# A graph layer's edge bookkeeping with one operand of each VectorE instruction in PSUM

## The chip, the cores and the metric

The kernel runs on one core of one Trainium2 chip. The metric is the device time of one execution in microseconds; before the change the median of three runs is 3950.51 us (3949.45 to 3950.6).

## What is computed

12,500 nodes with 128 features each and 200,000 edges, sorted by their destination. A node's row is normalized and passed through a relu; two graph layers follow, and their result is added to x:

```python
w = edge_weight_raw / jnp.maximum(wsum, EPS)[dst]
feat = jax.nn.relu(node_features @ W_pool + b_pool)
msg = feat[src] * w[:, None]
neigh = jax.ops.segment_max(msg, dst, num_segments=N)
...
rst = node_features @ W1_self + neigh @ W1_neigh + b1
...
h = jax.nn.relu(rst)
msg2 = h[src] * w[:, None]
neigh2 = jax.ops.segment_sum(msg2, dst, num_segments=N) / jnp.maximum(deg, 1.0)[:, None]
out = jax.nn.relu(h @ W2_self + neigh2 @ W2_neigh + b2)
```

Layer 1 takes the largest message of each destination, layer 2 their mean. The sums over a destination's edges (wsum, deg) and the places where one destination ends and the next begins have to be found from dst.

## The kernel before

The edges are cut into 391 groups of 512 (the last has 320), and 128 groups stand in one tile, so there are NT = 4 tiles of [128, 512]: one row of a tile is one group. The program has three stages.

**Preparation.** A loop over 25 sets of four 128-row node tiles, 28 turns with i from 0 to 27, is pipelined by hand. In one turn VectorE adds the bias of set i-3 (`fb`, line 388), forms the reciprocal and offset of set i-1 (403, 405) and the statistics of set i (420, 421); ScalarE normalizes (`xn`, line 409, four instructions), takes the square root (423) and copies the transposed set into `hT` (396); PE transposes (411) and multiplies by W_pool (399); GpSimd does the relu (`fr`, 391); SP stores the rows in the table `feat_d` in HBM (392). Between turns the loop draws single steps from generators: the edge work of tile 0 (`edges1`, one step per turn from i=2), loads, and `sources` (371, 374), which lays the source indices out as `srcT`.

**Layer 1** is a loop over groups, again pipelined by hand. In turn i GpSimd issues up to four gathers (`indirect_dma_start`, line 525), each of 128 rows of `feat_d` by a column of `srcT`; their tiles `gt` come from a pool of eight buffers. In every twelfth group one chunk of 128 rows is fetched row by row from the queues of SP and ScalarE instead (`Rows`, lines 459 to 517, tile `ga`). ScalarE scales the rows by the edge weight (`gs`, 654), PE transposes them into `pm` (655), VectorE runs the maximum along each row with a scan (661: `pm` in PSUM, `kt` in SBUF) in which `kt`, a broadcast row of `keep_d`, cuts the run at a new destination. Lines 669 and 670 draw pairs together, 678 builds a selection matrix, 685, 698, 703 and 710 place the result in `agg`, and `nodes1` (555 to 580) turns a finished node tile into rows of `h_d`, the table of layer 2.

Beside that loop runs the **edge work**: `edges1` (tiles 1 to 3; tile 0 was done in the preparation), `edges2`, `edges3`, `fitness` for all four tiles, and `verdict`, in that order. `edges1` marks where a destination goes on (`goes`) and ends (`last`), writes `keep_d`, sums the weights of each destination with two scans (231, 239: the second starts from the carry of the row before), and forms `ewT`, `lastT`, `invT` and `bases`. `edges2` counts edges, forms the place within the window (`locT`) and the reciprocal of weight times count; `edges3` scans backwards and forms `w2T`, the weights of layer 2; `fitness` tests whether the edge list suits the fast path. Each is a generator; a `yield` ends a step. The lists of steps are worked off by `side_step`, one step at a time, at the end of each odd turn:

```python
            if i % 2:
                side_step()
```

A job with a due turn is finished at once when its turn has come; everything else is due at turn 391. Each VectorE operation of these jobs works on [128, 512] or half of it; nearly all two-input ones read two tensors in SBUF. The only PSUM tile that they use is `pq`, of which the preparation has two buffers and layer 1 one.

**Layer 2** gathers rows of `h_d` with the same line 525 and sums them with matmuls (759) whose weights come from `locT` and `w2T`.

[...]

Of the kernel before, what the change touches and what calls it, by code (L numbers as in the profile page):

```python
# [8 lines left out]
BF16 = mybir.dt.bfloat16  # L9
# [3 lines left out]
AF = mybir.ActivationFunctionType  # L13
OP = mybir.AluOpType
AX = mybir.AxisListType
# [3 lines left out]
P = 128  # L19
D = 128  # L20
G = 512
Q = 4
# [13 lines left out]
def gnn_kernel(ctx, tc, x, src, dst, ew, w_pool, b_pool, w1s, w1n, b1, w2s, w2n, b2, out):  # L36
# [155 lines left out]
    def work(name, n=G, dtype=F32):  # L192
        return rp.tile([P, n], dtype, name=f"r_{name}")

    def columns(get, f, n):

        pt = get()
        for j in range(n):
            nc.tensor.transpose(pt[:, j, :], f[:, j * P:(j + 1) * P], ident)
        return pt[:, :n, :]  # L200

    def carried(get, a, t, near, wrap, step):

        pe = get()[:, 0, 0:1]
        nc.tensor.matmul(pe, shift[near], a[:, t + 1:t + 2], start=True, stop=False)
        nc.tensor.matmul(pe, shift[wrap], a[:, t + 1 + step:t + 2 + step], start=False, stop=True)
        return pe

    def backwards(a):
        return bass.AP(tensor=a.tensor, offset=a.offset + G - 1, ap=[list(a.ap[0]), [-1, G]])  # L210

    def pairs(a):
        return a.rearrange("p (c two) -> p c two", two=2)

    def edges1(get, t):

        before, cur, behind = (dr[:, t, i:i + G] for i in range(3))
        begin = work("first", 1)
        nc.vector.tensor_copy(begin, cur[:, 0:1])
        pe = get()[0:1, 0, :]  # L220
        nc.tensor.matmul(pe, begin, ident, start=True, stop=True)
        goes = work("goes", dtype=BF16)
        nc.vector.tensor_tensor(goes, cur, before, OP.is_equal)
        keep = work("keep", dtype=BF16)
        nc.vector.tensor_scalar(keep, goes, 1.0, -NEG, op0=OP.subtract, op1=OP.mult)
        nc.sync.dma_start(keep_d[t * P:(t + 1) * P, :], keep)
        yield
        nc.vector.tensor_copy(bases[0:1, t * P:(t + 1) * P], pe)
        pt = columns(get, er[:, t, :], Q)
        fw = work("f0")  # L230
        nc.vector.tensor_tensor_scan(fw, goes, er[:, t, :], 0.0, op0=OP.mult, op1=OP.add)
        nc.vector.tensor_copy(sums[:, t + 1:t + 2], fw[:, G - 1:G])
        yield
        nc.scalar.activation(ewT[:, t], pt, AF.Copy)
        pe = carried(get, sums, t, "up", "up_wrap", -1)
        yield
        first = work("first", 1)
        nc.vector.tensor_copy(first, pe)
        nc.vector.tensor_tensor_scan(fw, goes, er[:, t, :], first, op0=OP.mult, op1=OP.add)
        yield  # L240
        last = work("last", dtype=BF16)
        nc.vector.tensor_tensor(last, cur, behind, OP.not_equal)
        yield
        nc.vector.tensor_tensor(er[:, t, :], fw, last, OP.mult)
        yield
        loc = work("f1")
        nc.vector.tensor_tensor(loc, cur, cur[:, 0:1].to_broadcast([P, G]), OP.subtract)
        yield
        nc.vector.scalar_tensor_tensor(loc, loc, 1.0, last, op0=OP.add, op1=OP.mult)
        yield  # L250
        two, inv = fw[:, :G // 2], fw[:, G // 2:]
        nc.vector.tensor_tensor(two, pairs(loc)[:, :, 0], pairs(loc)[:, :, 1], OP.max)
        nc.vector.tensor_tensor(inv, pairs(er[:, t, :])[:, :, 0], pairs(er[:, t, :])[:, :, 1], OP.add)
        yield
        nc.vector.tensor_scalar(inv, inv, TINY, None, op0=OP.max)
        pt = columns(get, two, Q // 2)
        yield
        nc.vector.reciprocal(inv[:, :G // 4], inv[:, :G // 4])
        yield
        nc.scalar.activation(lastT[:, t], pt, AF.Copy)  # L260
        yield
        nc.vector.reciprocal(inv[:, G // 4:], inv[:, G // 4:])
        pt = columns(get, inv, Q // 2)
        yield
        nc.scalar.activation(invT[:, t], pt, AF.Copy)

    def edges2(get, t):

        before, cur, behind = (dr[:, t, i:i + G] for i in range(3))
        goes = work("goes", dtype=BF16)  # L270
        nc.vector.tensor_tensor(goes, cur, before, OP.is_equal)
        yield
        fw = work("f0")
        nc.vector.tensor_tensor_scan(fw, goes, ones_r, 0.0, op0=OP.mult, op1=OP.add)
        nc.vector.tensor_copy(counts[:, t + 1:t + 2], fw[:, G - 1:G])
        yield
        pe = carried(get, counts, t, "up", "up_wrap", -1)
        loc = work("f1")
        nc.vector.tensor_tensor(loc, cur, cur[:, 0:1].to_broadcast([P, G]), OP.subtract)
        yield  # L280
        first = work("first", 1)
        nc.vector.tensor_copy(first, pe)
        nc.vector.tensor_tensor_scan(fw, goes, ones_r, first, op0=OP.mult, op1=OP.add)
        pt = columns(get, loc, Q)
        yield
        nc.scalar.activation(locT[:, t], pt, AF.Copy)
        yield
        nc.vector.scalar_tensor_tensor(fw, er[:, t, :], TINY, fw, op0=OP.max, op1=OP.mult)
        yield
        for j in range(Q):  # L290
            nc.vector.reciprocal(fw[:, j * P:(j + 1) * P], fw[:, j * P:(j + 1) * P])
            yield
        last = work("last", dtype=BF16)
        nc.vector.tensor_tensor(last, cur, behind, OP.not_equal)
        yield
        nc.vector.tensor_tensor(er[:, t, :], fw, last, OP.mult)

    def edges3(get, t):

        cur, behind = (dr[:, t, i:i + G] for i in (1, 2))  # L300
        stays = work("goes", dtype=BF16)
        nc.vector.tensor_tensor(stays, cur, behind, OP.is_equal)
        yield
        bw = work("f0")
        nc.vector.tensor_tensor_scan(backwards(bw), backwards(stays), backwards(er[:, t, :]), 0.0,
                                     op0=OP.mult, op1=OP.add)
        nc.vector.tensor_copy(heads[:, t + 1:t + 2], bw[:, 0:1])
        yield
        pe = carried(get, heads, t, "down", "down_wrap", 1)
        yield  # L310
        first = work("first", 1)
        nc.vector.tensor_copy(first, pe)
        nc.vector.tensor_tensor_scan(backwards(bw), backwards(stays), backwards(er[:, t, :]), first,
                                     op0=OP.mult, op1=OP.add)
        pt = columns(get, bw, Q)
        yield
        nc.vector.tensor_tensor(w2T[:, t], pt, ewT[:, t], OP.mult)

    def fitness(get, t):

        before, cur, behind = (dr[:, t, i:i + G] for i in range(3))
        begin = cur[:, 0:1]
        wrong = work("goes", dtype=BF16)
        nc.vector.tensor_tensor(wrong, cur, before, OP.is_lt)
        yield
        nc.vector.tensor_reduce(bad[:, t, 0:1], wrong, axis=AX.X, op=OP.max)
        yield
        loc = work("f1")
        nc.vector.scalar_tensor_tensor(loc, cur, float(N - 1), begin.to_broadcast([P, G]),
                                       op0=OP.min, op1=OP.subtract)  # L330
        yield
        nc.vector.tensor_scalar(wrong, loc, float(LW - 1), None, op0=OP.is_gt)
        yield
        nc.vector.tensor_reduce(bad[:, t, 1:2], wrong, axis=AX.X, op=OP.max)
        yield

        one = work("first", 1)
        nc.vector.tensor_tensor(one, before[:, 0:1], behind[:, G - 1:G], OP.is_equal)
        real = work("real", 1)
        nc.vector.tensor_scalar(real, begin, float(PAST), None, op0=OP.is_lt)  # L340
        nc.vector.tensor_tensor(bad[:, t, 2:3], one, real, OP.mult)
        nc.vector.tensor_tensor(bad[:, t, 3:4], begin, need[:, t:t + 1], OP.is_lt)
        yield

        last = work("last", dtype=BF16)
        nc.vector.tensor_tensor(last, cur, behind, OP.not_equal)
        yield
        nc.vector.tensor_tensor(wrong[:, :G // 2], pairs(last)[:, :, 0], pairs(last)[:, :, 1], OP.mult)
        nc.vector.tensor_reduce(bad[:, t, 4:5], wrong[:, :G // 2], axis=AX.X, op=OP.max)

    def verdict(get):
        all_bad = work("first", 1)
# [30 lines left out]
    for i in range(len(groups) + 3):  # L383
# [29 lines left out]
        if at[0]:  # L413
# [9 lines left out]
            nc.scalar.activation(rstd, mv[:, :, 1], AF.Sqrt, bias=eps)  # L423
            offs[i] = ps.tile([P, Q], F32, name="neg")
            nc.vector.tensor_scalar(offs[i], mv[:, :, 0], -1.0, None, op0=OP.mult)
        if 2 <= i < 20:
            next(first_edges, None)
        if i >= 6:
            next(rest, None)
# [174 lines left out]
    with tc.manual_schedule(), tc.tile_pool(name="ew", bufs=3) as wk, \  # L604
# [33 lines left out]
        for i in range(max(turn) + 6):  # L638
# [72 lines left out]
                                     stop=j == len(chunks) - 1)  # L711
            node_stage(2)
            byrow.rows(i, nc.scalar)
            if i % 2:
                side_step()
        assert not busy
        i = NG
# [168 lines left out]
```

## Time and profile before

| what | value |
| --- | --- |
| median of 3 runs | 3950.51 us |
| the profiled execution's own time | 3949.8 us |
| its span | 3947.9 us |
| first and last gather of layer 1 | 91.9 and 2023.9 us |
| first and last gather of layer 2 | 2045.8 and 3936.5 us |
| busy: PE, PE weight loads | 55%, 45% of the span |
| busy: VectorE, ScalarE | 42%, 20% |
| busy: GpSimd | 75% |
| mean granted TensorE clock | 0.529 |
| DMA: bytes moved, mean rate | 295.43 MB, 75 GB/s |

A row of the profile's groups gives line, engine and operation, what is written and read by the program's names, the shapes and the count; then the busy time in us and the mean duration in ns; then the idle time of the engine just before, and what ended most of it. GpSimd's busy time does not count the time in which it issues: "issue" stands for a pause in which the engine waited for nothing that the profile shows. In the timeline a row begins with the start in us from the span's start and the duration in us; the bracket tells how long the engine was idle before it, and what ended that. In the chain of work that ended last, each piece has a start and a duration, and is followed by what it released.

### The profile page before, as it was taken

Reading aid. Unit: us, or ns where it says so; the run is one execution under the profiler, and the core shown is the slowest. Engines: PE = TensorE matmul, PEld = TensorE weight load, DVE = VectorE, ACT = ScalarE, POOL = GpSimd, SP = SyncE. Lnnn points to the kernel's source line nnn. Section 1 sums busy time; section 2 is a strip of 40 time slices with the busy share of each in tenths; the row PEclk is TensorE's granted clock in tenths of the full one; section 3 lists DMA queues with packets and bytes.
Section 4 is the critical chain, followed back from the end, with each engine's and each line's share of the span. In section 5 each row is a group of like instructions: output and inputs, shape, how many; then the busy total and the mean of one; then the engine's idle time right before and its main releaser. Section 6 shows DMA issues by size and latency. Waiting matters only on the chain.

```text
span 3947.9 us, 55088 instructions
## 1 busy us (share of the span) xinstructions
PE 2163.9 (55%) x8349; PEld 1764.2 (45%) x8349; DVE 1664.7 (42%) x4700; ACT 795.0 (20%) x2907; POOL 2946.2 (75%) x3105
## 2 busy tenths in 40 slices
PE   6546546546555455445555555555555555555555
PEld 4335445435444344344444444444444444444444
DVE  7556656657656656556552222121221222222221
ACT  6334334334334334334320000000000000000000
POOL 5777777777777777777757777777777777777776
PEclk8555555555555555555555555555555555555555
DMA  6233333333333333333322222222222222222222
GB/s 170 75 83 85 84 84 84 84 83 82 84 84 82 85 85 84 85 86 83 86 65 61 62 63 61 62 62 62 62 62 62 62 62 62 62 62 62 62 62 58
DMA packets 245792, 295.43 MB, mean 75 GB/s; under 512 B 71023, under 2 KB 195518, under 8 KB 245424
## 3 DMA queue, kind: packets, MB, share of 16 engines
q0 software_dynamic: 97472, 199.75, 18.8%
q1 hardware_dynamic: 139024, 89.04, 8.4%
q10 hardware_dynamic: 8928, 3.03, 0.3%
q14 instruction: 296, 2.42, 0.2%
q8 instruction: 72, 1.18, 0.1%
HBM read 271.77 MB, written 19.77 MB: 74 GB/s over the span
## 4 chain that ended last, share of the span: by engine, by line
DMA 24%; POOL 23%; issue 17%; SPq 10%; PE 9%; DVE 7%; ACT 5%; ACTq 4%; POOLq 0%; DVEq 0%
POOL gt L525 23%; DMA gt<-h_d,srcT 14%; SPq L514 6%; PE pm L655 4%; DMA kt<-keep_d 4%; DVE pm L661 4%; DMA ga<-feat_d 3%; ACTq L514 3%; ACT gs L654 3%; SPq L510 2%; DMA ri<-in_src 1%; DMA gt<-feat_d,srcT 1%; PE pa L710 1%; SPq L625 1%; PE pn L552 1%
## 5 line engine op out<-in xcount | busy, mean ns | idle before, releaser
L525 POOL DMA_INDIRECT gt<-feat_d,srcT x1531 | 1466.1, 958 | 469.5 <-issue 391.4
L525 POOL DMA_INDIRECT gt<-h_d,srcT x1515 | 1429.5, 944 | 483.1 <-issue 388.3
L759 PE MATMUL pa<-s,gt 128*128 128x48 f32 x3030 | 967.9, 423 | 826.6 <-DMA gt<-h_d,srcT 736.1
L759 PEld LDWEIGHTS pa<-s,gt 128*128 128x128 f32 x3030 | 757.5, 312 | 1038.6 <-DMA gt<-h_d,srcT 818.6
L655 PE MATMUL pm<-ident,gs 128*128 128x128 f32 x1563 | 484.0, 439 | 902.0 <-DVE sc L670 497.3
L655 PEld LDWEIGHTS pm<-ident,gs 128*128 128x128 f32 x1563 | 288.5, 199 | 1038.2 <-issue 483.4
L764 DVE TENSOR_TENSOR agg<-pa,agg 128x48 f32 x391 | 81.2, 208 | 1439.3 <-PE pa L759 1025.7
L661 DVE TENSOR_TENSOR_SCAN pm<-kt,carry,pm 128x512 f32<-128x512 bf16 x390 | 499.3, 1280 | 255.1 <-DMA kt<-keep_d 118.2
L654 ACT ACTIVATE gs<-gt,ewT 128x128 f32<-128x128 f32 x1531 | 503.6, 392 | 357.0 <-DMA ga<-feat_d 200.6
L710 PEld LDWEIGHTS pa<-sel,rows 128*128 128x128 f32 x1564 | 352.5, 311 | 35.9 <-ACT agg L703 34.0
L710 PE MATMUL pa<-sel,rows 128*128 128x48 f32 x1564 | 358.0, 375 | 2.6 <-ACT agg L703 1.1
L698 PE MATMUL pr<-ident,sc 128*128 128x128 f32 x782 | 236.3, 403 | 0.8 <-DVE sc L670 0.7
L500 DVE TENSOR_SCALAR ri<-ri 1x128 int32<-1x128 int32 x80 | 18.2, 227 | 505.1 <-DMA ri<-in_src 495.7
L678 DVE TENSOR_SCALAR sel<-cols,lastT,invT 128x48 f32<-128x48 f32 x782 | 213.0, 327 | 0.0
L670 DVE COPY_PREDICATED sc<-kt,pm 128x256 f32<-128x256 int16 x391 | 173.0, 443 | 13.3
L698 PEld LDWEIGHTS pr<-ident,sc 128*128 128x128 f32 x782 | 163.0, 218 | 1.2 <-PE pa L710 1.0
L669 DVE COPY sc<-pm 128x256 f32<-128x256 f32 x391 | 162.0, 414 | 0.0
L741 DVE TENSOR_TENSOR s<-hit,w2T 128x192 f32<-128x192 f32 x391 | 139.8, 357 | 13.5
L685 ACT ACTIVATE rows<-pr 128x256 f32<-128x256 f32 x392 | 142.3, 363 | 2.2 <-PE pr L698 2.2
L739 DVE TENSOR_TENSOR hit<-iota,locT 128x192 f32<-128x192 f32 x391 | 139.1, 356 | 0.8
L703 ACT ACTIVATE agg<-pa 128x48 f32 x391 | 78.5, 201 | 162.4 <-PE pn L553 157.0
L565 ACT ACTIVATE sq<-r 128x128 f32<-128x128 f32 x98 | 29.7, 303 | 375.7 <-DVE r L561 375.7
(144 smaller groups left out, 1374.0 us busy)
## 6 DMA issues: line engine op xcount, KB each, us to landing
kt<-keep_d SPq DMA_DIRECT2D x390, 128.0 KB
ga<-feat_d SPq DMA_DIRECT2D x3072, 0.5 KB
ga<-h_d SPq DMA_DIRECT2D x3072, 0.5 KB
ga<-h_d ACTq DMA_DIRECT2D x3072, 0.5 KB
gt<-feat_d,srcT POOLq DMA_INDIRECT x1531
gt<-h_d,srcT POOLq DMA_INDIRECT x1515
ga<-feat_d ACTq DMA_DIRECT2D x1024, 0.5 KB
h_d<-h SPq DMA_DIRECT2D x98, 64.0 KB
```

What stands on the lines that cost most here:

```text
L514: eng.dma_start(ga[r + k:r + k + 1, :], self.bytes[None, bass.ds(at[k], 4 * D)])
L525: nc.gpsimd.indirect_dma_start(out=gt[:k, j, :], out_offset=None, in_=table_d[:, :], in_offset=bass.IndirectOffsetOnAxis(ap=srcT[:k, t, j, ...
L654: nc.scalar.activation(gs[:k, j, :], rows_j, AF.Copy, scale=ewT[:k, t, j, r:r + 1])
L655: nc.tensor.transpose(pms[i][:, j * P:j * P + k], gs[:k, j, :], ident[:k, :k])
L661: nc.vector.tensor_tensor_scan(pm[:, :ne], kt[:, :ne], pm[:, :ne], carry, op0=OP.add, op1=OP.max)
L669: nc.vector.tensor_copy(sc[:, :ne // 2], two[:, :, 1])
L670: nc.vector.copy_predicated(sc[:, :ne // 2], new[:, :, 1], two[:, :, 0])
L678: nc.vector.tensor_scalar(sels[g][:k, j, :], cols[:k, 1, :], lastT[:k, t, j, r:r + 1], invT[:k, t, j, r:r + 1], op0=OP.is_equal, op1=OP.mult)
L685: nc.scalar.activation(rws[g][:k, j, :], pr[:k, j, :], AF.Copy)
L698: nc.tensor.transpose(prs[g][:k, j, :], sc[:, j * P:j * P + k], ident)
L710: nc.tensor.matmul(pas[g], rows[:k, j, :], sel[:k, j, :], start=j == 0, stop=j == len(chunks) - 1)
L759: nc.tensor.matmul(pas[g], rows_j, s[:k, j, :], start=j == 0, stop=j == len(chunks) - 1)
```

## The change

The difference lies in the edge work and in when it is drawn:

- `beside` takes a PSUM tile and has ScalarE copy an SBUF tensor of 512 columns into it. `edges1`, `edges2`, `edges3` and `fitness` read that copy as one operand, and the other one stays in SBUF. The scans write in place in PSUM; the reciprocals of `edges2` write to PSUM too.
- Maxima and sums over pairs of columns, formerly two strided operands of `tensor_tensor`, become a `tensor_reduce` over one tensor (`at_pairs`).
- `edges1` forms `loc` in one operation instead of two, with the row's first destination less one as a scalar per partition (`less`).
- There are more, shorter steps. Layer 1 takes a step in each turn that three does not divide, and the preparation draws from `edges1` in two more turns (to i=21).

```diff
+    def beside(get, f):
+        pt = get().rearrange("p q n -> p (q n)")
+        nc.scalar.activation(pt, f, AF.Copy)
+        return pt
+    def at_pairs(out, f, op):
+        nc.vector.tensor_reduce(out, pairs(f), axis=AX.X, op=op)
...
     def edges1(get, t):
...
+        less = work("real", 1)
+        nc.vector.tensor_scalar(less, begin, 1.0, None, op0=OP.subtract)
+        pn = beside(get, cur)
+        yield
         goes = work("goes", dtype=BF16)
-        nc.vector.tensor_tensor(goes, cur, before, OP.is_equal)
+        nc.vector.tensor_tensor(goes, pn, before, OP.is_equal)
...
+        nc.vector.tensor_tensor(last, pn, behind, OP.not_equal)
+        yield
+        loc = work("f1")
+        nc.vector.scalar_tensor_tensor(loc, pn, less, last, op0=OP.subtract, op1=OP.mult)
...
-        nc.vector.tensor_tensor_scan(fw, goes, er[:, t, :], 0.0, op0=OP.mult, op1=OP.add)
-        nc.vector.tensor_copy(sums[:, t + 1:t + 2], fw[:, G - 1:G])
+        pw = beside(get, er[:, t, :])
+        yield
+        nc.vector.tensor_tensor_scan(pw, goes, pw, 0.0, op0=OP.mult, op1=OP.add)
+        nc.vector.tensor_copy(sums[:, t + 1:t + 2], pw[:, G - 1:G])
...
-        nc.vector.tensor_tensor_scan(fw, goes, er[:, t, :], first, op0=OP.mult, op1=OP.add)
-        yield
-        last = work("last", dtype=BF16)
-        nc.vector.tensor_tensor(last, cur, behind, OP.not_equal)
-        yield
-        nc.vector.tensor_tensor(er[:, t, :], fw, last, OP.mult)
-        yield
-        loc = work("f1")
-        nc.vector.tensor_tensor(loc, cur, cur[:, 0:1].to_broadcast([P, G]), OP.subtract)
-        yield
-        nc.vector.scalar_tensor_tensor(loc, loc, 1.0, last, op0=OP.add, op1=OP.mult)
+        pw = beside(get, er[:, t, :])
+        yield
+        nc.vector.tensor_tensor_scan(pw, goes, pw, first, op0=OP.mult, op1=OP.add)
+        yield
+        nc.vector.tensor_tensor(er[:, t, :], pw, last, OP.mult)
         yield
+        fw = work("f0")
         two, inv = fw[:, :G // 2], fw[:, G // 2:]
-        nc.vector.tensor_tensor(two, pairs(loc)[:, :, 0], pairs(loc)[:, :, 1], OP.max)
-        nc.vector.tensor_tensor(inv, pairs(er[:, t, :])[:, :, 0], pairs(er[:, t, :])[:, :, 1], OP.add)
+        at_pairs(two, loc, OP.max)
+        yield
+        at_pairs(inv, er[:, t, :], OP.add)
...
     def edges2(get, t):
...
+        nc.vector.tensor_scalar(loc, pn, begin, None, op0=OP.subtract)
...
+        pc = beside(get, ones_r)
+        yield
+        nc.vector.tensor_tensor_scan(pc, goes, pc, 0.0, op0=OP.mult, op1=OP.add)
...
+        pr = get().rearrange("p q n -> p (q n)")
         for j in range(Q):
-            nc.vector.reciprocal(fw[:, j * P:(j + 1) * P], fw[:, j * P:(j + 1) * P])
+            nc.vector.reciprocal(pr[:, j * P:(j + 1) * P], fw[:, j * P:(j + 1) * P])
             yield
...
-        if 2 <= i < 20:
+        if 2 <= i < 22:
             next(first_edges, None)
...
-            if i % 2:
+            if i % 3:
                 side_step()
```

`edges3` and `fitness` are changed in the same way: a copy of the destinations, and in `edges3` of `er` ahead of each of the two scans, goes into PSUM and is read there.

More of the change, by code (lines that the diff above doesn't have):

```diff
@@ L219, in edges1 @@
         nc.vector.tensor_copy(begin, cur[:, 0:1])
-        pe = get()[0:1, 0, :]
-        nc.tensor.matmul(pe, begin, ident, start=True, stop=True)
+        less = work("real", 1)
+        nc.vector.tensor_scalar(less, begin, 1.0, None, op0=OP.subtract)
+        pn = beside(get, cur)
+        yield
         goes = work("goes", dtype=BF16)
-        nc.vector.tensor_tensor(goes, cur, before, OP.is_equal)
+        nc.vector.tensor_tensor(goes, pn, before, OP.is_equal)
         keep = work("keep", dtype=BF16)
@@ L227, in edges1 @@
         yield
+        last = work("last", dtype=BF16)
+        nc.vector.tensor_tensor(last, pn, behind, OP.not_equal)
[3 more added lines that the diff above has]
+        yield
+        pe = get()[0:1, 0, :]
+        nc.tensor.matmul(pe, begin, ident, start=True, stop=True)
+        yield
         nc.vector.tensor_copy(bases[0:1, t * P:(t + 1) * P], pe)
         pt = columns(get, er[:, t, :], Q)
-        fw = work("f0")
-        nc.vector.tensor_tensor_scan(fw, goes, er[:, t, :], 0.0, op0=OP.mult, op1=OP.add)
-        nc.vector.tensor_copy(sums[:, t + 1:t + 2], fw[:, G - 1:G])
         yield
         nc.scalar.activation(ewT[:, t], pt, AF.Copy)
+        yield
[4 more added lines that the diff above has]
+        yield
         pe = carried(get, sums, t, "up", "up_wrap", -1)
@@ L238, in edges1 @@
         nc.vector.tensor_copy(first, pe)
-        nc.vector.tensor_tensor_scan(fw, goes, er[:, t, :], first, op0=OP.mult, op1=OP.add)
         yield
-        last = work("last", dtype=BF16)
-        nc.vector.tensor_tensor(last, cur, behind, OP.not_equal)
+        pw = beside(get, er[:, t, :])
         yield
-        nc.vector.tensor_tensor(er[:, t, :], fw, last, OP.mult)
+        nc.vector.tensor_tensor_scan(pw, goes, pw, first, op0=OP.mult, op1=OP.add)
         yield
-        loc = work("f1")
-        nc.vector.tensor_tensor(loc, cur, cur[:, 0:1].to_broadcast([P, G]), OP.subtract)
+        nc.vector.tensor_tensor(er[:, t, :], pw, last, OP.mult)
         yield
-        nc.vector.scalar_tensor_tensor(loc, loc, 1.0, last, op0=OP.add, op1=OP.mult)
+        fw = work("f0")
+        two, inv = fw[:, :G // 2], fw[:, G // 2:]
+        at_pairs(two, loc, OP.max)
         yield
-        two, inv = fw[:, :G // 2], fw[:, G // 2:]
-        nc.vector.tensor_tensor(two, pairs(loc)[:, :, 0], pairs(loc)[:, :, 1], OP.max)
-        nc.vector.tensor_tensor(inv, pairs(er[:, t, :])[:, :, 0], pairs(er[:, t, :])[:, :, 1], OP.add)
+        at_pairs(inv, er[:, t, :], OP.add)
+        pt = columns(get, two, Q // 2)
         yield
         nc.vector.tensor_scalar(inv, inv, TINY, None, op0=OP.max)
-        pt = columns(get, two, Q // 2)
-        yield
         nc.vector.reciprocal(inv[:, :G // 4], inv[:, :G // 4])
@@ L269, in edges2 @@
         before, cur, behind = (dr[:, t, i:i + G] for i in range(3))
+        begin = work("first", 1)
+        nc.vector.tensor_copy(begin, cur[:, 0:1])
+        pn = beside(get, cur)
+        yield
         goes = work("goes", dtype=BF16)
-        nc.vector.tensor_tensor(goes, cur, before, OP.is_equal)
+        nc.vector.tensor_tensor(goes, pn, before, OP.is_equal)
         yield
-        fw = work("f0")
-        nc.vector.tensor_tensor_scan(fw, goes, ones_r, 0.0, op0=OP.mult, op1=OP.add)
-        nc.vector.tensor_copy(counts[:, t + 1:t + 2], fw[:, G - 1:G])
+        last = work("last", dtype=BF16)
+        nc.vector.tensor_tensor(last, pn, behind, OP.not_equal)
         yield
-        pe = carried(get, counts, t, "up", "up_wrap", -1)
         loc = work("f1")
-        nc.vector.tensor_tensor(loc, cur, cur[:, 0:1].to_broadcast([P, G]), OP.subtract)
+        nc.vector.tensor_scalar(loc, pn, begin, None, op0=OP.subtract)
         yield
-        first = work("first", 1)
-        nc.vector.tensor_copy(first, pe)
-        nc.vector.tensor_tensor_scan(fw, goes, ones_r, first, op0=OP.mult, op1=OP.add)
         pt = columns(get, loc, Q)
@@ L287, in edges2 @@
         yield
-        nc.vector.scalar_tensor_tensor(fw, er[:, t, :], TINY, fw, op0=OP.max, op1=OP.mult)
+        pc = beside(get, ones_r)
         yield
+        nc.vector.tensor_tensor_scan(pc, goes, pc, 0.0, op0=OP.mult, op1=OP.add)
+        nc.vector.tensor_copy(counts[:, t + 1:t + 2], pc[:, G - 1:G])
+        yield
+        pe = carried(get, counts, t, "up", "up_wrap", -1)
+        yield
+        first = work("first", 1)
+        nc.vector.tensor_copy(first, pe)
+        yield
+        pc = beside(get, ones_r)
+        yield
+        nc.vector.tensor_tensor_scan(pc, goes, pc, first, op0=OP.mult, op1=OP.add)
+        yield
+        fw = work("f0")
+        nc.vector.scalar_tensor_tensor(fw, er[:, t, :], TINY, pc, op0=OP.max, op1=OP.mult)
+        yield
+        pr = get().rearrange("p q n -> p (q n)")
         for j in range(Q):
-            nc.vector.reciprocal(fw[:, j * P:(j + 1) * P], fw[:, j * P:(j + 1) * P])
+            nc.vector.reciprocal(pr[:, j * P:(j + 1) * P], fw[:, j * P:(j + 1) * P])
             yield
-        last = work("last", dtype=BF16)
-        nc.vector.tensor_tensor(last, cur, behind, OP.not_equal)
-        yield
-        nc.vector.tensor_tensor(er[:, t, :], fw, last, OP.mult)
+        nc.vector.tensor_tensor(er[:, t, :], pr, last, OP.mult)
     def edges3(get, t):
         cur, behind = (dr[:, t, i:i + G] for i in (1, 2))
+        pn = beside(get, cur)
+        yield
         stays = work("goes", dtype=BF16)
-        nc.vector.tensor_tensor(stays, cur, behind, OP.is_equal)
+        nc.vector.tensor_tensor(stays, pn, behind, OP.is_equal)
         yield
-        bw = work("f0")
-        nc.vector.tensor_tensor_scan(backwards(bw), backwards(stays), backwards(er[:, t, :]), 0.0,
+        pw = beside(get, er[:, t, :])
+        yield
+        nc.vector.tensor_tensor_scan(backwards(pw), backwards(stays), backwards(pw), 0.0,
                                      op0=OP.mult, op1=OP.add)
-        nc.vector.tensor_copy(heads[:, t + 1:t + 2], bw[:, 0:1])
+        nc.vector.tensor_copy(heads[:, t + 1:t + 2], pw[:, 0:1])
         yield
@@ L312, in edges3 @@
         nc.vector.tensor_copy(first, pe)
-        nc.vector.tensor_tensor_scan(backwards(bw), backwards(stays), backwards(er[:, t, :]), first,
+        yield
+        pw = beside(get, er[:, t, :])
+        yield
+        bw = work("f0")
+        nc.vector.tensor_tensor_scan(backwards(bw), backwards(stays), backwards(pw), first,
                                      op0=OP.mult, op1=OP.add)
+        yield
         pt = columns(get, bw, Q)
@@ L321, in fitness @@
         before, cur, behind = (dr[:, t, i:i + G] for i in range(3))
-        begin = cur[:, 0:1]
+        begin = work("first", 1)
+        nc.vector.tensor_copy(begin, cur[:, 0:1])
+        pn = beside(get, cur)
+        yield
         wrong = work("goes", dtype=BF16)
-        nc.vector.tensor_tensor(wrong, cur, before, OP.is_lt)
+        nc.vector.tensor_tensor(wrong, pn, before, OP.is_lt)
         yield
@@ L328, in fitness @@
         loc = work("f1")
-        nc.vector.scalar_tensor_tensor(loc, cur, float(N - 1), begin.to_broadcast([P, G]),
-                                       op0=OP.min, op1=OP.subtract)
+        nc.vector.tensor_scalar(loc, pn, float(N - 1), begin, op0=OP.min, op1=OP.subtract)
+        last = work("last", dtype=BF16)
+        yield
+        nc.vector.tensor_tensor(last, pn, behind, OP.not_equal)
         yield
@@ L335, in fitness @@
         yield
-        one = work("first", 1)
+        one = work("one", 1)
         nc.vector.tensor_tensor(one, before[:, 0:1], behind[:, G - 1:G], OP.is_equal)
@@ L343, in fitness @@
         yield
-        last = work("last", dtype=BF16)
-        nc.vector.tensor_tensor(last, cur, behind, OP.not_equal)
+        at_pairs(loc[:, :G // 2], last, OP.min)
         yield
-        nc.vector.tensor_tensor(wrong[:, :G // 2], pairs(last)[:, :, 0], pairs(last)[:, :, 1], OP.mult)
-        nc.vector.tensor_reduce(bad[:, t, 4:5], wrong[:, :G // 2], axis=AX.X, op=OP.max)
+        nc.vector.tensor_reduce(bad[:, t, 4:5], loc[:, :G // 2], axis=AX.X, op=OP.max)
     def verdict(get):
```

## The prediction

> **What bounds the kernel now.** I read the page's costliest groups first, then GpSimd's waits, then the share of each stretch, then the timeline around single gathers. The page's rows of the two gathers (line 525):
>
> ```profile
> L525 POOL DMA_INDIRECT gt<-feat_d,srcT x1531 | 1466.1, 958 | 469.5 <-issue 391.4
> L525 POOL DMA_INDIRECT gt<-h_d,srcT x1515 | 1429.5, 944 | 483.1 <-issue 388.3
> ```
>
> 3046 gathers are busy for 2895.6 us and each has about 0.30 us of its own issue ahead of it, so GpSimd alone makes some 3810 us of the 3947.9 us span. Layer 1's mean is 958 ns against 944 ns in layer 2: 14 ns x 1531 = 21 us. GpSimd's waits in layer 1 (92 to 2040 us) show nothing longer than the pause that every gather has, except the 2.7 us ahead of the first:
>
> ```profile
> POOL gt L525 <- issue: 391.4, 1275, 2.7
> POOL gt L525 <- DMA gt<-feat_d,srcT: 46.1, 151, 0.3
> POOL gt L525 <- ACT gs L654: 19.8, 65, 0.3
> ```
>
> GpSimd never waits for a buffer or a consumer between two gathers. So a gather made shorter ends layer 1 earlier by the same amount, and so does a first gather that starts earlier. Where the 21 us sit, by GpSimd's busy time in stretches (the columns are window, length, busy, count):
>
> ```profile
> 500.00:1000.00 500.00, 379.62 (x395) 0.55 0.33 84
> 1400.00:2000.00 600.00, 453.33 (x481) 0.54 0.33 85
> 2500.00:3900.00 1400.00, 1057.82 (x1122) 0.50 0.22 62
> ```
>
> That is 961, 942 and 943 ns. Side steps (lines 215 to 349) run until about 1372 us; after that the excess is gone. One gather beside one side step:
>
> ```profile
> 112.34 1.99 POOL L525 DMA_INDIRECT gt<-feat_d,srcT  x1 [0.30 <-issue]
> 112.37 1.20 DVE L231 TENSOR_TENSOR_SCAN r_f<-r_goes,er 128x512 f32<-128x512 bf16 x1
> ```
>
> The scan ends at 113.57, the gather 0.75 us later. Laying every gather's record over VectorE's: where a side instruction with two tensors in SBUF covers about the 190th ns of a gather, the gather ends 0.75 us after a scan or 0.82 us after another operation, instead of 0.94 us after its own start. Layer 1 has 83 such instructions (22 scans of 1248 ns, the rest of about 680 or 420 ns), and 50 gathers are hit. Summed over lines 223 to 346, the excess over 944 ns is **20.3 us**: the scans of lines 231, 239, 274, 283, 305 and 313 9.8 us, the others 10.5. The counterexample is the scan of the main loop, equally long, with one tensor in SBUF and one in PSUM:
>
> ```profile
> 1500.52 0.94 POOL L525 DMA_INDIRECT gt<-feat_d,srcT  x1 [0.30 <-issue]
> 1500.52 1.29 DVE L661 TENSOR_TENSOR_SCAN pm<-kt,carry,pm 128x512 f32<-128x512 bf16 x1 [0.79 <-PE pm L655]
> 1501.77 0.94 POOL L525 DMA_INDIRECT gt<-feat_d,srcT  x1 [0.30 <-issue]
> ```
>
> 390 of those cost the gathers 0.04 us together. So it is the second SBUF tensor, not VectorE's activity.
>
> **Part 1: the operand in PSUM, layer 1.** Every side operation over 512 columns with two tensors in SBUF gets one from PSUM. At most the 20.3 us go; the small hits of `sel` (line 678, 0.6 us over 19 gathers), of `copy_predicated` (0.2) and of the lines 255 and 332 (0.2) stay, as those are not changed. Lower bound of the gain: 0, if the stall came from something else.
>
> [...] by the rows it is 20.3 us. I take the rows: the gather has srcT as an input, and its extra time ends with the VectorE instruction.
>
> The copies: 37 of `beside` in layer 1 at about 0.59 us (nearest rows: line 234, 588 ns, and line 286, 596 ns; from bf16 or int32 no row, bounds 0.58 to 0.60 by line 374), 22 us on ScalarE, which is busy 37% there. They and the longer chain of steps delay the consumers, not GpSimd. The cover is the eight gather buffers (some 39 us of gathers): from the end of `gs` of group g to the first gather of group g+8, which takes its buffer, I find at least 14.6 us in the records of lines 654 and 525, 26 us in the median. Only a lag of more would cost, then one to one.
>
> VectorE: operands in PSUM cost no more (line 317 with PSUM 683 ns, line 244 without 684). Per tile, edges1 loses one 0.68 us operation, gains a 0.15 us one, and its two pair operations go from 0.42 to about 0.68 each (line 334's reduction over 512); the other jobs change by less than 0.4. Sum near 0, and hidden anyway. Reciprocals and backward scans with PSUM have no row; I take their 945 and 1215 to 1284 ns; twice that would be hidden too.
>
> **Part 2: two of three turns.** Steps: before 3x13+4x11+4x4+4x7+1 = 128, at every second turn, done by turn 256 (1372 us as seen). After 3x19+4x17+4x9+4x9+1 = 198, at two of three turns: turn 297, about 1560 us, before the loop's 391 groups end (260 are to be had). Nothing is left for the end, where it would delay layer 2. keep_d of a tile stands two steps into its job, well before its rows are read. Cost 0.
>
> **Part 3: tile 0's steps in the preparation.** They ran at i=2 to 15 and now take i=2 to 21 of 28. The first gather (91.9 us) follows the last feat_d store, so this stage is on the path. Its chain has two regimes: from 21 to 48 us at a granted clock of 0.50 the loop is 3.6 us long through PE (line 399 2.07, line 411 0.87, hT 0.61), with VectorE and ScalarE free for 0.5 to 1.2 us; from 49 to 89 us at 1.00 the loop takes 2.69 us and VectorE is full. There a step lies on the chain:
>
> ```profile
> 54.37 0.42 PE pt L411 x3
> 54.79 0.01 issue
> 54.81 0.94 DVE r_f L262
> 55.75 0.54 DVE fb L388
> ```
>
> and the next hT came 3.5 instead of 2.7 us later: 0.85 of 0.94 us was paid. Before, the five loops around 49 us (46.7 to 61.4) held L262 and two ScalarE copies and took 14.7 instead of 13.45: +1.3. After, i=13 to 21 hold: a ScalarE copy of 0.59; the second scan 1.28; the product with `last` 0.68; two reductions 0.68 each; max and reciprocal 0.39+0.94; a copy 0.37; reciprocal 0.94; a copy 0.36. VectorE 5.6 us paid at 0.9 is 5.0, copies at about 0.35 each 1.0, together 6.0: **+4.7** against before. In the first 21 us line 231 (1.20, with 228 and 232 1.6) goes later and 0.97 takes its place, and ewT leaves (0.38 on the chain): -0.8. In the 0.50 stretch PE's four transposes of er and the carried pair wait behind hT's 0.6 us: +0.3. Sum **+4.3 us**. Bounds: +1 if waits of the stage that I take for full hide more, +7 if each step is paid in full and the stage runs past 89.5 us into the slow clock.
>
> **Sum.** 3949.8 (the profiled execution, span 3947.9) - 20.3 + 4.3 = 3933.8; the median of the runs is 0.7 above the profiled execution: **3934.5 us**. The tail of layer 1 (2024 to 2046 us) and layer 2 stay, as nothing in them changes.
>
> **The rivals.**
> - A, chance 0.60, 3931 to 3938: the sum above.
> - B, 0.15, 3928 to 3931: the preparation hides the later steps. 3950.5 - 20.3 + 0 to 1. For: the 0.50 stretch hides all. Against: the chain lines at 54.8 us.
> - C, 0.10, 3938 to 3946: part of the stalls stays, for example for operations whose [128,1] scalar lies in SBUF beside an SBUF tensor, or new ones come from reductions. Half of 20.3 left: 3950.5 - 10 + 4.3 = 3944.8. Against: line 661 has such a scalar (carry) and stalls nothing; reductions (lines 326 and 334) hit no gather.
> - D, 0.11, slower: the lock is the result's way into SBUF[...], so all stalls stay and only Part 3 acts: 3950.5 + 4.3 = 3954.8, at its upper bound 3958. It decides if side operations with PSUM sources but SBUF results still stretch gathers to over 1.2 us. Against: line 669 and line 678 write SBUF all the time without it.
> - E, 0.04: consumers lag by more than 14.6 us, since ScalarE's copy waits in its queue for the one pq buffer while gs and the row loads stand behind it; each us beyond is paid, 3960 and more. Against: the lag of 24 us after each late row tile is made up within twelve turns.
>
> A measurement of this kernel can tell about 0.2% (8 us) from no change. Faster by more (under 3942.6): A, B and two thirds of C, 0.82; within: the rest of C and D, 0.14; slower: E, 0.04. The range, 3928 to 3944, takes in A, B and most of C.
>
> **What would show it.** Right: the mean of line 525's successor in layer 1 falls to 944 or 945 ns, no gather over 1.3 us behind 92 us; the first gather starts at about 96 us; steps end near 1560 us; ScalarE has 40 copies of 0.59 us. Wrong: gathers of 1.2 us and more beside the new operations (C, D), pauses of more than 0.3 us between gathers (E), or a first gather at 92 us (B).

## The result and the profile after

The changed kernel takes 3938.58 us (median of nine runs, 3935.86 to 3941.1) against 3950.14 us (3948.66 to 3953.25, nine runs) before: a ratio of 0.9971 [0.9962, 0.998], 11.6 us less. The forecast was 3934.5 us, 16 us less. The profiled execution of the changed kernel took 3936.91 us with a span of 3935.1 us, so 12.8 us less than the one before.

The page's rows of the two gathers, now line 567:

```profile
L567 POOL DMA_INDIRECT gt<-feat_d,srcT x1531 | 1446.1, 945 | 469.5 <-issue 376.4
L567 POOL DMA_INDIRECT gt<-h_d,srcT x1515 | 1429.5, 944 | 487.3 <-issue 389.5
```

Layer 1's gathers are as short as layer 2's: 1466.1 has become 1446.1 us, at the same idle sum. GpSimd's busy time in the stretches (window, length, busy, count):

```profile
500.00:1000.00 500.00, 377.81 (x400) 0.55 0.32 85
1400.00:2000.00 600.00, 453.57 (x481) 0.54 0.32 85
2500.00:3900.00 1400.00, 1057.72 (x1122) 0.50 0.22 62
```

The stretch from 500 to 1000 us held 395 gathers of 961 ns and now holds 400 of 945. Beside the side scan of `edges1` that writes in place in PSUM (line 265), the timeline shows what the main loop's scan showed before:

```profile
486.46 1.28 DVE L265 TENSOR_TENSOR_SCAN pq<-r_goes,r_first,pq 128x512 f32<-128x512 bf16 x1
486.47 0.94 POOL L567 DMA_INDIRECT gt<-feat_d,srcT  x1 [0.30 <-issue]
487.65 1.26 DVE L703 TENSOR_TENSOR_SCAN pm<-kt,carry,pm 128x512 f32<-128x512 bf16 x1
487.72 0.94 POOL L567 DMA_INDIRECT gt<-feat_d,srcT  x1 [0.30 <-ACT gs L696]
```

The scan covers the whole gather, and the gather takes 0.94 us. Summed over the layer, the excess over 944 ns fell from 22.3 to 2.25 us, most of it in gathers that a `sel` operation overlaps; no gather takes 1.3 us or more, where 28 did before. GpSimd's waits from 92 to 2040 us (total, times, longest):

```profile
POOL gt L567 <- issue: 378.0, 1239, 0.3
POOL gt L567 <- ACT gs L696: 25.9, 85, 0.3
POOL gt L567 <- DMA ri<-in_src: 25.2, 1, 25.2
POOL gt L567 <- DMA feat_d<-fr: 2.8, 1, 2.8
```

Only two are longer than a gather's own pause, and they stand at the two borders of the layer: the first gather, and the first one of layer 2. The first is in GpSimd's timeline:

```profile
95.30 1.16 POOL L567 DMA_INDIRECT gt<-feat_d,srcT  x1 [2.75 <-DMA feat_d<-fr]
```

It was at 91.9 us. The second is the layer's tail, which GpSimd's timeline of the kernel before shows like this:

```profile
2023.88 0.91 POOL L525 DMA_INDIRECT gt<-feat_d,srcT  x1 [0.30 <-issue]
2045.80 0.96 POOL L525 DMA_INDIRECT gt<-h_d,srcT  x1 [21.01 <-DMA ri<-in_src]
```

and that of the kernel after like this:

```profile
2007.19 0.91 POOL L567 DMA_INDIRECT gt<-feat_d,srcT  x1 [0.30 <-issue]
2033.27 0.95 POOL L567 DMA_INDIRECT gt<-h_d,srcT  x1 [25.17 <-DMA ri<-in_src]
```

The last gather of layer 1 comes 16.7 us earlier, the first of layer 2 only 12.5 us: the pause between them grew by 4.2 us. Layer 2 took 1891.6 us in both. So the terms are -20.0 (gathers) + 3.4 (first gather) + 4.2 (tail) = -12.4 us, of the -12.8 us between the profiled executions. Two terms were forecast; the third was not.

### The profile page after: what moved, and what is told of

It is laid out like the page before. It is cut to its first block, busy times and chain, and to the rows that moved or that the text cites. A ratio compares the mean times of both kernels' runs of the same rounds, so it can differ in the third digit from the quotient of the medians.

```text
span 3935.1 us, 55137 instructions
## 1 busy us (share of the span) xinstructions
PE 2156.9 (55%) x8349; PEld 1760.9 (45%) x8349; DVE 1664.5 (42%) x4708; ACT 808.7 (21%) x2947; POOL 2925.7 (74%) x3105
## 3 DMA queue, kind: packets, MB, share of 16 engines
q0 software_dynamic: 97472, 199.75, 18.7%
## 4 chain that ended last, share of the span: by engine, by line
DMA 23%; POOL 23%; issue 17%; SPq 9%; PE 9%; DVE 8%; ACT 5%; ACTq 5%; POOLq 0%; DVEq 0%
POOL gt L567 23%; DMA gt<-h_d,srcT 14%; SPq L556 6%; PE pm L697 4%; DVE pm L703 4%; ACTq L556 3%; DMA ga<-feat_d 3%; DMA kt<-keep_d 3%; ACT gs L696 3%; SPq L552 2%; DMA ri<-in_src 1%; ACTq L552 1%; PE pa L752 1%; DMA gt<-feat_d,srcT 1%; SPq L667 1%
## 5 line engine op out<-in xcount | busy, mean ns | idle before, releaser
L567 POOL DMA_INDIRECT gt<-feat_d,srcT x1531 | 1446.1, 945 | 469.5 <-issue 376.4
L696 ACT ACTIVATE gs<-gt,ewT 128x128 f32<-128x128 f32 x1531 | 495.6, 391 | 269.0 <-DMA ga<-feat_d 187.7
L542 DVE TENSOR_SCALAR ri<-ri 1x128 int32<-1x128 int32 x80 | 18.6, 233 | 512.3 <-DMA ri<-in_src 504.7
L783 DVE TENSOR_TENSOR s<-hit,w2T 128x192 f32<-128x192 f32 x391 | 139.8, 357 | 13.5
```

What stands on the lines that cost most here:

```text
L567: nc.gpsimd.indirect_dma_start(out=gt[:k, j, :], out_offset=None, in_=table_d[:, :], in_offset=bass.IndirectOffsetOnAxis(ap=srcT[:k, t, j, ...
L696: nc.scalar.activation(gs[:k, j, :], rows_j, AF.Copy, scale=ewT[:k, t, j, r:r + 1])
```

## The experiments

My theory behind the first four: the stall needs two tensors of one VectorE instruction in SBUF; the later first gather comes from tile 0's longer list of steps; the longer tail comes from how far the consumers lag at the last groups. Rivals: the stall hangs on the result's way (rival D), and the tail comes from ScalarE's copies standing in its queue (rival E's mechanism, with a price only at the layer's end).

These four ran on a chip where the kernel before took 5863.65 us (5849.72 to 5881.36). There eight row loads of SP in layer 1 took 5.4 to 5.5 us in the mean and up to 19.6 us, against 3.2 and at most 9.0 us in the kernel before on the chip of the result. GpSimd waits for the consumers again and again, for some 1000 us more in layer 1's gathers than in the kernel before on the chip of the result. What such a chip can tell is therefore the length of single gathers and the preparation, not what a stall costs.

### Both inputs of the scans in SBUF, the results in PSUM

```diff
-        nc.vector.tensor_tensor_scan(pw, goes, pw, 0.0, op0=OP.mult, op1=OP.add)
+        nc.vector.tensor_tensor_scan(pw, goes, er[:, t, :], 0.0, op0=OP.mult, op1=OP.add)
```

The same in the other forward scans (`er` or `ones_r` in place of the copy) and the backward ones; the copies stay. Five of the six scans write to PSUM; the second one of `edges3` writes to SBUF here and in the changed kernel.

> The six scans read er or ones_r from SBUF beside goes, their results still go where they go after the change (five into PSUM); the copies stay in the program, though the scans don't read them. Theory 'second SBUF input': the scans' share of the stalls comes back, 9.8 us by the trace of before[...], the gathers of layer 1 take 1456 us and single ones reach 2.0 us; at the end of layer 1 some of it is given back, since the tail after the last gather should fall from 25.2 us towards 21. Time 3944 to 3948. Theory 'the result's way into SBUF': results stay in PSUM, so no stall, 1446 us and 3938.

Measured: 5829.49 us, ratio 0.9945 [0.9923, 0.9966]. The time tells nothing on that chip: the page's row has 1493.0 us of idle time, which would cover any stall.

```profile
L567 POOL DMA_INDIRECT gt<-feat_d,srcT x1531 | 1449.9, 947 | 1493.0 <-ACT rows L727 998.4
```

The timeline tells:

```profile
271.38 1.28 DVE L265 TENSOR_TENSOR_SCAN pq<-r_goes,r_first,er 128x512 f32<-128x512 bf16 x1
271.44 1.96 POOL L567 DMA_INDIRECT gt<-feat_d,srcT  x1 [0.30 <-issue]
```

This is the scan of line 265 again, with its result in PSUM as in the changed kernel; only its second input is in SBUF. The gather ends at 273.40, 0.74 us after the scan, as in the kernel before. 33 gathers exceed 960 ns, and their excess over 944 ns is 6.2 us, 5.0 of it in 12 gathers beside the six changed scans; in the other three kernels it is 1.1 to 1.5 us in all. That is half of the 9.8 us expected, which 17 gathers beside the scans made up before. So for the scans it is the second SBUF input that stalls the gather, and not the result's way.

### VectorE makes layer 1's copies

```diff
-        nc.scalar.activation(pt, f, AF.Copy)
+        if get is pq:
+            nc.scalar.activation(pt, f, AF.Copy)
+        else:
+            nc.vector.tensor_copy(pt, f)
```

> After the change, but in layer 1 VectorE makes the copies into PSUM (one SBUF input, PSUM output) and ScalarE none, so ScalarE never waits in its queue for the PSUM buffer. Stalls as after the change: 1446 us of gathers[...]. Theory 'ScalarE's queue' (the tail grew because its copy waited 18 us for w2T behind VectorE's wait for a row of indices): the tail from the last gather's end to layer 2 is 21 to 22 us and the time 3935. Theory 'row loads bound' (the consumers, paced by SP's row loads, can't keep up with a GpSimd that doesn't stall): the tail stays at 25 us or a little more, time 3938 to 3940.

Measured: 5820.73 us, 0.9929 [0.9909, 0.9948]; tail 55.2 us, against 56.2 and 56.3 us in the two kernels of this set that leave the copies and the row groups as they are. No difference to see on that chip.

### The last row-loaded group is gathered whole

```diff
-            for g in range(every, NG - 4, every):
+            for g in range(every, self.end, every):
...
-        byrow = Rows(wk, feat_d, 12, [(nc.sync, 96, 8), (nc.scalar, 32, 4)])
+        byrow = Rows(wk, feat_d, 12, [(nc.sync, 96, 8), (nc.scalar, 32, 4)], keep=16)
```

Here `self.end` is NG - keep, and `keep` is 4 elsewhere: group 384, six groups ahead of the last, is no longer fetched by row, at the price of one more gather (1.25 us with its pause).

> After the change, but group 384 of layer 1, the last one that gets 128 rows one by one, is gathered whole: 31 groups with row loads instead of 32, one gather more (1.25 us). If the tail of layer 1 is set by the lag that the last row group leaves, as both theories say, the lag at the last group falls from 7.1 us to about 2 and the tail from 25.2 to 19 or 20 us: 4 us faster than the changed kernel, 3934 to 3935. If the tail is set by anything else (the last node tiles, the stores), it stays at 25 and the time is 3940.

Measured: 5804.79 us, 0.9894 [0.987, 0.9918]; the tail is 36.2 us. So 20 us of this chip's tail, 56.2 us with group 384 loaded by row, come with that group.

### The old steps of tile 0 in the preparation

```diff
-    first_edges = edges1(pq, 0)
+    first_edges = edges1_plain(pq, 0)
...
-        if 2 <= i < 22:
+        if 2 <= i < 20:
```

`edges1_plain` is `edges1` of the kernel before; layer 1 keeps the new steps.

> After the change, but tile 0's edge work in the preparation is done as before (two SBUF operands, steps at i=2 to 15); tiles 1 to 3 and all later jobs as after. If the later steps are what delays the first gather, it starts at 91.9 us instead of 95.3, and the time falls by 3.4 us to 3935; if the delay came from elsewhere (the granted clock's switch), the first gather stays at 95.

Measured: 5828.13 us, 0.9935 [0.9914, 0.9955]. The first gather is at 91.16 us, against 95.26, 94.05 and 94.42 us in the other three. The preparation's term is the step list's.

### The same three on another chip, and two of them together

Here the kernel before took 3956.64 us (3947.74 to 3958.98, ten runs). `e_best` combines the old preparation with the last row group gathered whole.

> The same kernel as e_copies_dve, on another chip: on the first one, SP's row loads ran so slowly that the kernel before took 5864 us, and GpSimd waited for its buffers. Where the kernel before takes 3950 us: theory 'ScalarE's queue': the tail from the last gather's end of layer 1 to layer 2 is 21 to 22 us, time 3935. Theory 'row loads bound': the tail stays at 25 us or more, time 3938 to 3940.

> The same kernel as e_last_rows, on another chip. Where the kernel before takes 3950 us: both theories say that the tail is set by the lag that the last row group leaves: lag at the last group about 2 us instead of 7.1, tail 19 or 20 instead of 25.2 us, one gather more (1.25 us), so 3934 to 3935. If the tail is set by anything else, 3940.

> The same kernel as e_plain_prep, on another chip. On the first chip its first gather started at 91.2 us, with the later steps at 94.0 and 94.4. Where the kernel before takes 3950 us: first gather at 91.9 us, time 3935; if the delay came from elsewhere, first gather at 95 and 3938.5.

> Both together: tile 0's edge work in the preparation as before, and group 384 of layer 1 gathered whole. If the terms add, 3938.6 - 3.4 - 4 = 3931, which beats both kernels: ratio to before 0.9952. If the tail and the preparation share their cause, 3934 to 3935.

| kernel | median us | ratio | first gather us | tail us |
| --- | --- | --- | --- | --- |
| copies by VectorE | 3943.1 | 0.9969 [0.9957, 0.9981] | 95.6 | 20.6 |
| last row group gathered | 3938.28 | 0.9955 [0.9941, 0.9968] | 95.7 | 18.7 |
| old preparation | 3938.34 | 0.9954 [0.994, 0.9967] | 91.4 | 21.8 |
| both of these | 3936.05 | 0.995 [0.9937, 0.9964] | 91.8 | 18.7 |

Against the kernel before, the four are 13.5, 18.4, 18.3 and 20.6 us faster. The second and third did better than the 15 to 16 us expected, and together they gain only 2 us more than each alone, so their gains do not add. The first lies between what its two theories expected and decides nothing by its time. The first gather and the tail are those of each kernel's profiled execution. The old preparation starts 3.9 us before the changed kernel's profile; in its GpSimd timeline:

```profile
91.37 1.16 POOL L620 DMA_INDIRECT gt<-feat_d,srcT  x1 [2.74 <-issue]
```

The copies on VectorE bear on ScalarE's queue. With ScalarE's copies, at 1113 us, the changed kernel's timeline has the event that rival E was about:

```profile
1109.46 0.26 DVE L542 TENSOR_SCALAR ri<-ri 1x128 int32<-1x128 int32 x1 [15.98 <-DMA ri<-in_src]
1112.39 0.68 DVE L356 TENSOR_TENSOR w2T<-pq,ewT 128x512 f32<-128x512 f32 x1
1113.11 0.60 ACT L218 ACTIVATE pq<-dr 128x512 f32<-128x512 int32 x1 [18.17 <-DVE w2T L356]
```

VectorE waits 16 us for a load of indices, `w2T` behind it is late, so the one pq buffer stays taken and ScalarE's copy blocks its queue for 18 us. The consumers then lag by 20 us, but have made it up by about turn 240, and GpSimd never pauses. With the copies on VectorE that lag is 2.7 us at the same place. The tail is 20.6 us there, but the kernel with the old preparation has the event and a tail of 21.8: the event does not make the tail. Nor is the kernel faster than the changed one, by its ratio. That ScalarE's copies add nothing at all to the tail is not shown, with one profile of each.

### The changed kernel again, beside the best

> The changed kernel once more. In its first profile the tail of layer 1, from the end of the last gather to layer 2's first, was 25.2 us, and the lag at the last row group (384) 22.1 us; with VectorE's copies 20.6 and 17.5, with the old preparation 21.8 and 18.6, though that kernel's layer 1 is the same as this one's. Theory 'systematic' (a later start and the copies on ScalarE shift the row loads): the tail is 25 again, the time about 3.5 us above the old preparation's plus its 3.5, 3938.5. Theory 'scatter' (the lag of the last row group varies from one execution to the next by some us): the tail is anywhere from 20.5 to 25, the other terms repeat (gathers 1446 us, first at 95.5).

> The same kernel as e_best, on the chip and in the rounds of the changed kernel. Its tail has no row group to scatter: 18.7 us as in e_best. Against the changed kernel: preparation 3.5 us earlier, tail 2 to 6 us shorter, one gather (1.25 us) more, so 4 to 8 us less than after_b.

On one chip, where the kernel before took 3949.11 us (3944.05 to 3952.41): the changed kernel 3937.82 us (3933.15 to 3945.09), 0.9976 [0.9966, 0.9986]; the combination 3928.28 us (3928.01 to 3932.33), 0.9951 [0.9937, 0.9965]. The intervals do not meet, and the difference is 9.5 us: on this chip the combination beats both kernels. From 4 to 8 us were expected; the two profiled executions are 4.9 us apart. The changed kernel's second profile, from GpSimd's timeline:

```profile
93.82 1.16 POOL L567 DMA_INDIRECT gt<-feat_d,srcT  x1 [2.75 <-DMA feat_d<-fr]
...
2005.90 0.91 POOL L567 DMA_INDIRECT gt<-feat_d,srcT  x1 [0.30 <-issue]
2029.49 0.95 POOL L567 DMA_INDIRECT gt<-h_d,srcT  x1 [22.68 <-DMA ri<-in_src]
```

and that of the combination:

```profile
2004.67 0.91 POOL L621 DMA_INDIRECT gt<-feat_d,srcT  x1 [0.30 <-issue]
2024.26 0.96 POOL L621 DMA_INDIRECT gt<-h_d,srcT  x1 [18.68 <-DMA ri<-in_src]
```

The same kernel had its first gather 1.5 us and its tail 2.5 us lower than in its first profile. Both borders scatter from one execution to the next. This execution's own time, 3933.15 us, is also the lowest of its nine.

### The change with the scattering tail taken out of both sides

> The kernel before, with group 384 of layer 1 gathered whole: the tail of layer 1 without a last row group, which was 18.7 us in all three such kernels so far. The tail falls from 21.0 to 18.7, one gather (1.25 us) more: 1 us less than before, with less scatter. If the tail of before is not set by the row group, it stays at 21 and the time rises by 1.2 us.

> The changed kernel with group 384 gathered whole, beside the kernel before with the same edit. With the scattering tail taken out of both, the change is worth its other two terms: gathers 20.0 us shorter, first gather 3.4 us later, so 16.6 us (15 to 18) less than e_before_last. If the tail differs for another reason, the difference is 12 to 13 us.

On one chip again (before 3955.62 us, 3950.88 to 3962.75): the kernel before with the last row group gathered 3955.56 us, 0.9998 [0.999, 1.0006]; the changed kernel with it 3938.74 us, 0.9958 [0.9945, 0.9972]. The difference is 16.8 us. In GpSimd's timeline of the former

```profile
2030.88 0.91 POOL L526 DMA_INDIRECT gt<-feat_d,srcT  x1 [0.30 <-issue]
2049.70 0.96 POOL L526 DMA_INDIRECT gt<-h_d,srcT  x1 [17.91 <-DMA ri<-in_src]
```

and of the latter

```profile
2011.07 0.91 POOL L568 DMA_INDIRECT gt<-feat_d,srcT  x1 [0.30 <-issue]
2030.56 0.96 POOL L568 DMA_INDIRECT gt<-h_d,srcT  x1 [18.58 <-DMA ri<-in_src]
```

the tails are within 0.7 us of each other. With the tail equal, the change is worth about what the prediction's sum gave it, 16 us. The two profiled executions are 19.0 us apart: the gathers of layer 1 take 1472.7 us in the former and 1450.6 us in the latter, 22.1 us less, and the first one starts 2.2 us later. So the stalls are not a constant of the kernel; 20.0 us went in one pair of profiles and 22.1 in the other. The edit alone gives the old kernel nothing that can be measured, where 1 us was expected: 3.1 us of tail less than in the profile of the kernel before on the chip of the result, one gather more. Executions differ in GpSimd's own pace, with the old edge work and with the new: layer 2 takes about 1891.5 or 1895.5 us. For both layers that is some 8 us, an estimate from mean gathers of 944 or 946.5 ns, 3046 of them. So times are compared with the kernel before on the same chip. The pace is no property of a chip: of the four profiles of the table, that of the old preparation has the faster one and the other three the slower. A median of few runs can carry a part of these 8 us.

## Why the prediction was nearly right

**The stall (part 1): right, cause and size.** 20.3 us were forecast to go, 20.0 went. For the scans, `e_scans_sbuf` shows which operand it is; for the other operations the changed kernel does. There, 57 gathers of layer 1 have their 190th ns covered by an operation of the edge work over 512 columns with an input in PSUM, and the longest takes 1.0 us; of the 55 that an operation with two SBUF inputs covered in the kernel before, 45 took longer than that. Scans are not alone in this: the rows of before had 10.5 us of stalls that were not a scan's, 8.2 of them beside `tensor_tensor`. One of these, from the timeline of the kernel before:

```profile
169.45 0.69 DVE L244 TENSOR_TENSOR er<-r_f,r_last 128x512 f32<-128x512 f32 x1
169.53 1.43 POOL L525 DMA_INDIRECT gt<-feat_d,srcT  x1 [0.30 <-issue]
```

By the measured time alone, 3938.58 us, the result lies in the band of rival C (3938 to 3946) and just above that of A (3931 to 3938). The trace tells them apart: C falls with the 2.25 us of excess that are left. Rival D falls with the changed kernel itself, where the same product reads PSUM and writes to SBUF beside a gather of 0.94 us:

```profile
490.21 0.94 POOL L567 DMA_INDIRECT gt<-feat_d,srcT  x1 [0.30 <-DMA gt<-feat_d,srcT]
490.24 0.68 DVE L267 TENSOR_TENSOR er<-pq,r_last 128x512 f32<-128x512 f32 x1
```

One sentence of the prediction goes too far: "So it is the second SBUF tensor, not VectorE's activity." In the changed kernel's second profile a gather is stalled beside an operation with one tensor in SBUF, which writes to SBUF, and ends 0.82 us after it:

```profile
1344.65 1.26 POOL L567 DMA_INDIRECT gt<-feat_d,srcT  x1 [0.30 <-DMA gt<-feat_d,srcT]
1344.67 0.42 DVE L376 TENSOR_SCALAR r_goes<-r_f 128x512 bf16<-128x512 f32 x1
```

The prediction counted this operation (332 in the kernel before) among the small hits that stay; there are four of them in the layer.

**The costs of the operations: right.** From the groups of the changed kernel by form, layer 1 only:

```profile
L325 DVE RECIPROCAL pq<-r_f 128x128 f32<-128x128 f32 x16 | 15.2, 952 | 0.0
L339 DVE TENSOR_TENSOR_SCAN pq<-r_goes,pq 128x512 f32<-128x512 bf16 x4 | 4.9, 1220 | 0.0
L222 DVE TENSOR_REDUCE r_f<-er 128x256 f32<-128x512 f32 x3 | 2.0, 676 | 0.0
```

A reciprocal into PSUM takes 952 ns (taken: 945), a backward scan there 1220 (1215 to 1284), a reduction over pairs 676 (680). ScalarE's copies take 598 ns (590), from int32, bf16 or f32 alike.

**The cadence (part 2): as forecast, by the trace alone.** The steps end at about 1560 us, and no gather waits for a step. It was not tried by itself.

**The preparation (part 3): right, and about 1 us too large.** The forecast was +4.3 us. Its own terms, 4.7 - 0.8 + 0.3, give 4.2, and with the durations named for the middle one (1.6 less 0.97, and 0.38) that one is -1.0, so 4.0. Over the eight profiles with the later steps the first gather is at 94.8 us in the mean (93.8 to 95.7), over the six with the old ones at 91.6 (91.2 to 91.9): +3.2 us. The steps lie on the chain as taken; from the changed kernel's chain of work, between the operations of the loop:

```profile
53.51 1.28 DVE pq L265
54.78 0.58 DVE fb L430
...
57.35 0.68 DVE er L267
58.03 0.60 DVE fb L430
...
60.62 0.68 DVE r_f L222
61.30 0.60 DVE fb L430
```

Each is followed at once by the `fb` of the stage, which the stores wait for. Rival B falls with that. What makes up the rest was not separated.

**The tail: the step that failed.** The prediction says: "The tail of layer 1 (2024 to 2046 us) and layer 2 stay, as nothing in them changes." Layer 2 stayed; the tail was 25.2 and 22.7 us in the two profiles of the changed kernel, against 21.0 us in the one profile of the kernel before. From the medians, -11.6 = -20.0 + 3.2 + x, it grew by about 5 us; with the interval of the ratio x is anything from 2 to 9, and a part of it may be GpSimd's pace, known for the profiled executions alone. The reasoning stands in part 1: "Only a lag of more would cost", meaning more than the 14.6 us that the gather buffers cover. That is true within the layer, where GpSimd never paused, though the least cover fell to 11.0 us; rival E falls with that. At the layer's end the first gather of layer 2 needs the last rows of `h_d`, so whatever the consumers lag there is paid in full, cover or not.

The chain of the changed kernel passes through group 384's row loads:

```profile
1998.66 1.41 DMA ga<-feat_d
...
2000.22 0.41 ACT gs L696
...
2030.78 1.53 DMA h_d<-h
```

By the records, `gs` of that group ends 22.1 us after its last gather, against 18.0 us before the change and 19.6 us in the changed kernel's second profile; with the copies on VectorE it is 17.5 us, with the old preparation 18.6. In these five profiles the tail is that lag plus 3.0 to 3.2 us. Counted from the end of that `gs`, layer 2 starts 31.7 to 31.9 us later in all eight profiles in which group 384 is loaded by row, those of the slow chip included. Where group 384 is gathered whole, its lag is 1.9 to 2.1 us and the tail 17.9 to 18.7 us in all five profiles off the slow chip, old edge work or new. So the path is shown: the lag of the last row-loaded group sets the tail and its scatter, and with it gone from both sides the medians come within 1 us of the sum, the profiled pair within 3.

Why that lag is larger after the change is argued only. Twelve groups of unstalled gathers take 58.7 us, and the consumers of the changed kernel took 58.9 us for twelve groups in the mean from group 12 to 384; while gathers were being stalled, twelve groups took 59 to 61 us. A faster GpSimd leaves its consumers nothing to catch up with. But the last 650 us of the kernel before were unstalled too, and the scatter of the lag is as large as the difference: with the new edge work in layer 1, tails from 20.6 to 25.2 us were seen, and the kernel before has one profile. So what decides the lag's size is open. So too is why the changed kernel's times scatter over 12 us on one chip and the combination's over 4.

## What to carry to other kernels

When a producer that sets the pace is sped up, its cover within the loop says nothing of the loop's end: look there for what the next stage waits for, and add the lag of the consumers to the path. Before moving an operand to PSUM, lay the two engines' records over each other and find which instructions are hit; here one of two SBUF inputs was enough to move, and nearly all of the 20 us came back. Where a longer list of steps is drawn in two stages, use it only in the stage that needs it: in the preparation there are no gathers to protect, and it cost 3 us.

## What the runs showed of the hardware

- Beside a scan with both inputs in SBUF a gather took 1.96 us where the scan wrote to PSUM (`e_scans_sbuf`) and 1.99 us where it wrote to SBUF (the kernel before); beside the main loop's equally long scan with one input in PSUM it took 0.94 us.
- One tensor in SBUF was enough for a stall: beside a `tensor_scalar` over 512 columns from SBUF to SBUF (f32 to bf16, 0.42 us) a gather took 1.26 us in place of 0.94.
- One chip ran the kernel before 1.48 times as long (5863.65 us against 3950.14), with eight row loads of SP at about 5.5 us in place of 3.2 in the mean; why is open. The four variants of the changed kernel were 0.6 to 1.1% faster than the kernel before there. As GpSimd waited for its consumers anyway (1493.0 us of idle time ahead of layer 1's gathers in `e_scans_sbuf`), the stalls are not known to be the reason; neither a profile of the kernel before nor a run of the changed kernel exists on that chip.
- The mean gather took 944 ns in some executions and 946.5 ns in others, both in kernels with hardly any stalls; over 3046 gathers that makes 7.6 us.
